# Moving two groups of transposes and turning the last two w2 products in a routed feed-forward kernel

## The chip, the core and the metric

The kernel runs on one core of one Trainium2 chip. A core has five engines with instruction queues of their own: TensorE (PE in the profile; PEld is its weight load) multiplies matrices and writes only to PSUM, a memory of eight banks of 512 fp32 values per partition; VectorE (DVE), ScalarE (ACT) and GpSimd (POOL) do elementwise work; SyncE (SP) issues DMA transfers, as POOL does for the indirect ones. Each engine runs its queue in order. The metric is the device time of one execution in microseconds (us). Less is better.

## The reference

Two layers work on x of shape (2, 1024, 512) in fp32. After every sublayer comes a layer norm of x plus the sublayer's output. Layer 0 is linear attention and a feed-forward with 4-bit weights, layer 1 is gated linear attention and a routed feed-forward. The change lies in the last of these, so only that is shown:

```python
scores = jnp.einsum('bsd,d->bs', hidden_states, router_weight) + router_bias[0]
top_scores, indices = jax.lax.top_k(scores, K)          # K = 512 of 1024 rows of a batch
weights = jax.nn.sigmoid(top_scores)
selected = jnp.take_along_axis(hidden_states, indices[:, :, None], axis=1)
h = jax.nn.gelu(jnp.einsum('bkd,df->bkf', selected, w1) + b1)      # 512 -> 2048
processed = jnp.einsum('bkf,fd->bkd', h, w2) + b2                  # 2048 -> 512
weighted = processed * weights[:, :, None]
out = flat.at[flat_idx].add(weighted.reshape(b * K, d))
...
x = _layernorm(x + _L1_ffn_ref(x, ...), axis=-1)
```

## The kernel before

The 2048 rows of x are four blocks of 512; two blocks are a batch of 1024. Everything lies in SBUF as tiles of 128 rows. A tile framework orders the instructions of each engine by when they were traced and what they depend on, and places the semaphores; `tc.issue_after(ins)` adds the order "behind `ins`" for the instructions of its block on `ins`'s engine. It is no wait of another engine. So the order on an engine is that of the scheduler, where nothing pins it.

*Routing* (`route`, a generator that is advanced with `next`). For each batch it has a column of scores (`score`) per 128 rows. Eight transposes (`rp`, L1320) spread them over all partitions, two ACT copies (L1321) make one row of 1024 scores. DVE then compares each of the eight columns with the row (L1329, L1332, L1335, the result in `cmp`) and counts how many are ahead: that is a row's rank. With the rank as an index, eight indirect DMAs (L1345, from POOL) scatter the rows of x into a DRAM buffer `picked`, where ranks of 512 and more fall away.

*Fetch* (`fetch`). One DMA (L1372, from SP) loads the 512 picked rows (`xs`); sixteen transposes (`xsTp`, L197), four to a bank, and four ACT copies (L1375) give them with the features on partitions. `sums_of_x` (L1382 to L1385) forms four sums T1 to T4 of them on DVE, since both feed-forward products are done by a scheme of seven half-size products instead of eight (Strassen's in Winograd's form).

*First product and gelu* (`hidden`, once for each of two batches). Four groups g of 512 hidden features; in each, seven products (`product`, L1407) of four fp32 matmuls of 128x256. A product goes to the next bank of `either_bank`, which takes one of the ring `mm_bank` (banks 0 to 3) and one of the ring `acc_bank` (banks 4 to 7) in turn; score rows and transposed rows take banks of the `mm` ring too. ACT takes the first product of a group (L1416), DVE adds the others (L1418 to L1424, and L1427 for the seventh), and ACT applies gelu (L1400) with the table load that comes before it. `beside[g]` holds functions that are traced behind a group's last sum: sums of w1 (`sums_of_w1`), the rest of the ranking of batch 1, and for group 3 of batch 0 `next_rows`, which fetches the rows of batch 1 and forms their sums.

*Second product* (`finish_ffn`, generator `steps(b)`). Again seven products (`add`, L1486, eight fp32 matmuls of 128x256 for each half r of a bank). At the end of a batch the fourth product, with T4, is added to p1 (L1561), and then rows are finished in tiles of 128: `to_x(i, half, y)` adds a half (256 columns) of tile i, weighted, to the row (L1532) and takes its statistics (L1533); `end(i)` aggregates these (L1537), normalises (`layernorm`: DVE L180, a power on POOL L181, DVE L183) and scatters the 128 rows to the output (L1539, indirect, from POOL). Tiles 1 and 3 need the fourth product, tiles 0 and 2 the third, with S1, which is last:

```python
nc.vector.tensor_add(p1, p1, product(of_h(b, 1, 1), of_T(T4)))
for r in range(2):
    ...
    end(2 * r + 1)
for r in range(2):
    p3 = either_bank("yp")
    add(p3, of_S(S1[b]), of_w2(1, 1), r)
    to_x(2 * r, 1, row_half(p3, r))
    end(2 * r)
```

[...]

Of the kernel before, what the change touches and what calls it, by code (L numbers as in the profile page):

```python
# [21 lines left out]
P = 128  # L22
# [51 lines left out]
def body(ctx: ExitStack, tc: tile.TileContext, a: dict, out: bass.AP):  # L74
# [627 lines left out]
    with tc.tile_pool(name="s2", bufs=1) as wk2:  # L702
# [137 lines left out]
        class Normed:  # L840
# [25 lines left out]
            def to_x(self, part):  # L866
                for i in part:
                    x = x_t[self.blk][:, i]
                    nc.gpsimd.tensor_add(x, x, self.y[:, i])
# [442 lines left out]
    def route(b, room):  # L1312

        s = score[b]
        row = room.rearrange("p k t -> p (k t)")[:, :T]
        for h in range(2):
            rp = mm_bank("rp")
            for i in range(4):
                col = s[:, 4 * h + i : 4 * h + i + 1]
                nc.tensor.transpose(rp[:, i * P : (i + 1) * P], col.to_broadcast([P, P]), ident)  # L1320
            nc.scalar.copy(row[:, h * 512 : (h + 1) * 512], rp)  # L1321
        cnt = sp.tile([P, 8, 3], F32, tag="cnt", name="cnt", bufs=1)
        nc.gpsimd.memset(cnt, 0.0)
        yield
        for i in range(8):
            col = s[:, i : i + 1]
            cmp = jk.tile([P, T], BF16, tag="junk", name="cmp")
            if i:
                nc.vector.tensor_scalar(  # L1329
                    cmp[:, : i * P], row[:, : i * P], col, None, ALU.is_ge, ALU.add, accum_out=cnt[:, i, 0:1]  # L1330
                )
            nc.vector.tensor_scalar(  # L1332
                cmp[:, i * P :], row[:, i * P :], col, None, ALU.is_gt, ALU.add, accum_out=cnt[:, i, 1:2]
            )
            nc.vector.scalar_tensor_tensor(  # L1335
                cmp[:, :P], row[:, i * P : (i + 1) * P], col, const("tril"), ALU.is_equal, ALU.mult,
                accum_out=cnt[:, i, 2:3],
            )
            yield
        rank = sp.tile([P, 8], F32, tag="rank", name="rank")  # L1340
        nc.vector.tensor_reduce(rank, cnt, AX.X, ALU.add)
        nc.vector.tensor_copy(index[b], rank)
        rows = []
        for i in range(8):
            ins = nc.gpsimd.indirect_dma_start(  # L1345
                out=picked[b][:, :],
                out_offset=bass.IndirectOffsetOnAxis(ap=index[b][:, i : i + 1], axis=0),
                in_=x_row[2 * b + i // 4][:, i % 4],
                in_offset=None,
                bounds_check=TOPK - 1,  # L1350
                oob_is_err=False,
            )
            apart(ins.ins, rows)
        yield
# [13 lines left out]
    def fetch(b, room=None):  # L1368

        xs = xT_tile("xs")  # L1370
        room = room or xT_tile("xsT")
        nc.sync.dma_start(out=xs, in_=picked[b].rearrange("(c p) d -> p c d", p=P)[:, :, :C])  # L1372
        for i in range(4):
            pt = transposed(xs[:, i], "xsTp")
            nc.scalar.copy(room[:, :, i * P : (i + 1) * P], pt.rearrange("p (k t) -> p k t", k=KC))  # L1375
        return xs, room
# [8 lines left out]
        nc.vector.tensor_sub(T3, B22, B12)  # L1385
        return (B11, B21, B22), (T1, T2, T3, T4)

    turns = [0]

    def either_bank(name):  # L1390
        turns[0] += 1
        return (mm_bank, acc_bank)[turns[0] % 2](name)

    def hidden(b, xs, h, beside):

        (B11, B21, B22), (T1, T2, T3, T4) = xs

        def gelu(f):
            x = h[f // 4][:, f % 4]
            nc.scalar.activation(x, x, AF.Gelu_apprx_tanh, bias=b1[:, f : f + 1])  # L1400

        def product(w, g, x):

            ps = either_bank("hp")
            for j in range(2):
                for k in range(2):
                    nc.tensor.matmul(  # L1407
                        ps[:, 256 * j : 256 * j + 256], w[:, k, 2 * g + j], x[:, k], start=k == 0, stop=k == 1
                    )
            return ps.rearrange("p (j t) -> p j t", j=2)  # L1410

        for g in range(4):

            c = h[g].rearrange("p (j e) (s t) -> p j e s t", e=2, s=2)
            c11, c12, c21, c22 = (c[:, :, e, s] for e in range(2) for s in range(2))
            nc.scalar.copy(c11, product(wA11, g, B11))  # L1416
            p2 = product(wA12, g, B21)
            nc.vector.tensor_add(c12, c11, product(wS2, g, T2))  # L1418
            nc.vector.tensor_add(c11, c11, p2)
            nc.vector.tensor_add(c21, c12, product(wS3, g, T3))  # L1420
            p5 = product(wS1, g, T1)
            nc.vector.tensor_add(c22, c21, p5)
            nc.vector.tensor_add(c12, c12, p5)
            nc.vector.tensor_add(c12, c12, product(wS4, g, B22))  # L1424
            for j in range(2):
                gelu(4 * g + 2 * j)
            ins = nc.vector.tensor_sub(c21, c21, product(wA22, g, T4)).ins  # L1427
            for j in range(2):
                gelu(4 * g + 2 * j + 1)
            if g in beside:  # L1430
                with tc.issue_after(ins):
                    beside[g]()
# [5 lines left out]
    def finish_ffn(w2, h):  # L1438
# [33 lines left out]
        def of_h(b, e, s):  # L1472
            return lambda r, j: hv[b][j // 2][:, j % 2, e, r, s]

        def of_S(x):
            return lambda r, j: x[:, j, r]

        def of_w2(e, half):
            return lambda j: w2v[j // 2][:, j % 2, e, 256 * half : 256 * half + 256]

        def of_T(x):
            return lambda j: x[:, j]

        def add(ps, x, w, r):
            for j in range(NJ):
                nc.tensor.matmul(  # L1486
                    ps[:, 256 * r : 256 * r + 256], x(r, j), w(j), start=j == 0, stop=j == NJ - 1
                )

        def product(x, w):  # L1490
            ps = either_bank("yp")
            for r in range(2):
                add(ps, x, w, r)
            return ps
# [3 lines left out]
        def steps(b):  # L1498
# [14 lines left out]
            with tc.issue_after(ins):  # L1513
# [10 lines left out]
                for i in range(4):  # L1524
                    x = xs[:, i]
                    nc.vector.scalar_tensor_tensor(x, b2, weight[:, i : i + 1], x, ALU.mult, ALU.add)
            stats = sp.tile([P, 4, 2, 6], F32, tag="stats", name="stats", bufs=2)

            def to_x(i, half, y):

                x = xs[:, i, 256 * half : 256 * half + 256]
                nc.vector.scalar_tensor_tensor(x, y, weight[:, i : i + 1], x, ALU.mult, ALU.add)  # L1532
                nc.vector.bn_stats(stats[:, i, half], x)  # L1533

            def end(i):
                mv = sp.tile([P, 1, 2], F32, tag="mv4", name="mv4")
                nc.vector.bn_aggr(mv[:, 0], stats[:, i])  # L1537
                layernorm(xs[:, i : i + 1], mv, 0.25e-5)
                ins = nc.gpsimd.indirect_dma_start(  # L1539
                    out=out[:, :],  # L1540
                    out_offset=bass.IndirectOffsetOnAxis(ap=place[:, i : i + 1], axis=0),
                    in_=xs[:, i],
                    in_offset=None,
                    bounds_check=B * T - 1,
                    oob_is_err=False,
                )
                apart(ins.ins, scattered)

            def row_half(y, r):
                return y[:, 256 * r : 256 * r + 256]  # L1550
# [7 lines left out]
            nc.vector.tensor_add(c11, p1, p5)  # L1558
            nc.vector.tensor_add(u2, u2, p5)
            yield  # L1560
            nc.vector.tensor_add(p1, p1, product(of_h(b, 1, 1), of_T(T4)))  # L1561
            for r in range(2):
                x = xs[:, 2 * r, 256:]
                nc.vector.scalar_tensor_tensor(x, row_half(u2, r), weight[:, 2 * r : 2 * r + 1], x, ALU.mult, ALU.add)
                to_x(2 * r + 1, 1, row_half(c11, r))
                to_x(2 * r + 1, 0, row_half(p1, r))
                end(2 * r + 1)
            for r in range(2):
                p3 = either_bank("yp")
                add(p3, of_S(S1[b]), of_w2(1, 1), r)  # L1570
                to_x(2 * r, 1, row_half(p3, r))
                end(2 * r)
            yield

# [122 lines left out]
    def x_room(i, name):  # L1697
        return xpool.tile([P, 4, ROW], F32, tag=f"x{i}", name=name)[:, :, :C]
# [3 lines left out]
    def rank_some(n):  # L1702
        for _ in range(n):
            next(ranking, None)

    def next_rows():
        xs, x = fetch(1, room)
        later.append(xs)
        later.append(sums_of_x(x, x_room(0, "xsums")))

    rank_some(4)
    hidden(0, xs, h[0], {0: lambda: (sums_of_w1((2,)), rank_some(6)), 1: lambda: sums_of_w1((3,)), 3: next_rows})
    h.append([xT_tile("h10"), part(3, [4, 512], "h11"), later[0], x_room(1, "h13")])
    hidden(1, later[1], h[1], {g: lambda g=g: unpicked(g + 1) for g in range(3)})
    finish_ffn(w2, h)
# [52 lines left out]
```

## Time and profile before

| what | before |
|---|---|
| median of 3 runs | 979.3 us (979.05 to 979.5) |
| the profiled execution's own time | 979.27 us |
| its span in the profile | 977.5 us |
| granted TensorE clock, mean | 0.997 |
| PE busy | 962.0 us, 98% |
| DVE busy | 707.6 us, 72% |
| ACT busy | 289.2 us, 30% |
| POOL busy | 305.4 us, 31% |
| first product (`hp`, two batches) | 770.2 to 872.1 us |
| second product (`yp`) | 872.1 to 968.8 us |

The profile is of one execution; its span starts with its first instruction, and 1.77 us lie around it. Times in views are us from the start of the span unless marked ns. A line of the timeline has start, length, engine, line, operation, tiles and shapes, and at its end the engine's idle time before it with the instruction that ended it. The chain of waits follows the last instruction back to what released it at each step.

### The profile page before, as it was taken

The numbers are of one execution on the slowest core, as the hardware profiler recorded it, in microseconds if no ns is written. First come the engines' busy times: TensorE is split into PE (matmuls) and PEld (weight loads), VectorE is DVE, ScalarE is ACT, GpSimd is POOL, SyncE is SP. The second block draws the span as 40 slices with busy tenths as digits, with TensorE's granted clock in tenths as the row PEclk, the third lists the DMA queues.
The fourth block names the chain that finished last, engine by engine and source line by source line (L and its number), as shares of the span: only waits on it lengthen the run. The fifth ranks groups of instructions, "written<-read, shape, count | busy, mean of one in ns | idle before, by whom it ended". The sixth has DMA issues, their size and how long they took to land. (4 is left out here: it accounts for less than half of the span.)

```text
span 977.5 us, 11854 instructions
## 1 busy us (share of the span) xinstructions
PE 962.0 (98%) x4421; PEld 776.0 (79%) x4421; DVE 707.6 (72%) x1347; ACT 289.2 (30%) x496; POOL 305.4 (31%) x276
## 2 busy tenths in 40 slices
PE   9999999999999999999999999999999999999996
PEld 6668876775888888888888879969768688888885
DVE  3569986987975686686578396655887794898544
ACT  2344323333642263253243223232122123220000
POOL 1110283004887265575567012001042021000022
PEclk9999999999999999999999999999999999999998
DMA  9622222100000000000020410000014302140011
GB/s 323 208 84 79 88 67 67 49 1 1 1 1 1 1 1 1 1 1 1 0 87 1 177 60 1 2 0 2 0 39 147 117 22 66 44 172 0 1 44 44
DMA packets 25980, 48.87 MB, mean 50 GB/s; under 512 B 4684, under 2 KB 6732, under 8 KB 25411
## 3 DMA queue, kind: packets, MB, share of 16 engines
q1 hardware_dynamic: 23283, 42.98, 13.2%
q0 software_dynamic: 1920, 4.22, 1.1%
q10 hardware_dynamic: 720, 0.92, 0.3%
q8 instruction: 35, 0.57, 0.2%
q14 instruction: 22, 0.18, 0.1%
HBM read 39.70 MB, written 10.52 MB: 51 GB/s over the span
## 5 line engine op out<-in xcount | busy, mean ns | idle before, releaser
L181 POOL TENSOR_TENSOR rs<-rs,table 128x4 f32<-128x4 f32 (+1 forms) x21 | 19.8, 946 | 312.2 <-DVE rs L180 311.9
L741 DVE SCALAR_TENSOR_TENSOR gate<-gatep,scale,gate 128x512 f32<-128x512 f32 x123 | 91.3, 743 | 6.4 <-PE gatep L730 6.1
L741 DVE SCALAR_TENSOR_TENSOR up<-upp,scale,up 128x512 f32<-128x512 f32 x112 | 83.0, 741 | 0.1
L730 PE MATMUL gatep<-x1Th,wgu 128*128 128x512 f32 x176 | 72.5, 412 | 0.6 <-DVE x1Tl L212 0.6
L730 PE MATMUL upp<-x1Th,wgu 128*128 128x512 f32 x176 | 70.4, 400 | 0.1
L730 PE MATMUL upp<-x1Tl,wgu 128*128 128x512 f32 x176 | 68.9, 392 | 0.0
L730 PE MATMUL gatep<-x1Tl,wgu 128*128 128x512 f32 x176 | 68.9, 392 | 0.0
L735 ACT ACTIVATE gate<-gatep,scale 128x512 f32<-128x512 f32 x41 | 28.3, 691 | 110.3 <-PE gatep L730 104.0
L777 PE MATMUL P<-wdn,h 128*128 128x256 f32 x256 | 60.5, 379 | 0.0
L931 POOL TENSOR_TENSOR h<-up,gate 128x512 f32<-128x512 f32 x30 | 38.6, 1287 | 68.6 <-ACT gate L930 63.3
L777 PEld LDWEIGHTS P<-wdn,h 128*128 128x128 f32 x256 | 48.4, 190 | 6.7
L1133 POOL TENSOR_TENSOR sum<-sum,sq 128x512 f32<-128x512 f32 x12 | 17.3, 1442 | 90.7 <-issue 75.9
L1163 PE MATMUL go<-big 128*128 128x256 f32 x192 | 43.4, 380 | 0.0
L367 PE MATMUL xk<-pair,x 128*128 128x512 f32 x96 | 42.7, 592 | 0.0
L730 PEld LDWEIGHTS upp<-x1Th,wgu 128*128 128x128 f32 x176 | 33.0, 188 | 11.7 <-DVE up L741 3.4
L188 DVE BATCH_NORM_STATS2 st<-x 128x6 f32<-128x512 f32 x64 | 41.9, 673 | 0.4
L730 PEld LDWEIGHTS gatep<-x1Th,wgu 128*128 128x128 f32 x176 | 33.1, 188 | 9.2 <-DVE gate L741 1.9
L1163 PEld LDWEIGHTS go<-big 128*128 128x128 f32 x192 | 36.2, 190 | 4.8
L730 PEld LDWEIGHTS upp<-x1Tl,wgu 128*128 128x128 f32 x176 | 33.1, 188 | 6.4 <-issue 0.2
L730 PEld LDWEIGHTS gatep<-x1Tl,wgu 128*128 128x128 f32 x176 | 33.1, 188 | 6.0
L777 PE MATMUL P<-T,S 128*128 128x256 f32 x160 | 36.0, 379 | 0.0
L777 PEld LDWEIGHTS P<-T,S 128*128 128x128 f32 x160 | 30.3, 190 | 4.2
(484 smaller groups left out, 2325.1 us busy)
## 6 DMA issues: line engine op xcount, KB each, us to landing
pk<-in_gu SPq DMA_DIRECT2D x16, 352.0 KB, 3.8
x<-in_x SPq DMA_DIRECT2D x4, 1024.0 KB, 13.1
w<-in_w SPq DMA_DIRECT2D x1, 4096.0 KB, 13.9
xs<-picked SPq DMA_DIRECT2D x4, 1024.0 KB, 4.9
out<-x SPq DMA_DIRECT2D x4, 1024.0 KB, 4.3
w<-in_w SPq DMA_DIRECT2D x4, 1024.0 KB, 6.9
x0T<-in_xT SPq DMA_DIRECT2D x3, 1024.0 KB, 7.2
pk<-in_dn SPq DMA_DIRECT2D x11, 256.0 KB, 3.3
```

Source lines behind the costliest of these rows:

```text
L181: power = nc.gpsimd.tensor_tensor(rs[:, :n], rs[:, :n], const("mhalf")[:, :n], ALU.pow).ins
L188: nc.vector.bn_stats(st, x)
L367: ins = nc.tensor.matmul(acc_of[b][c], x_t[blk][:, i, c * P : (c + 1) * P], pairs_of["k", blk][i // 2][:, i % 2], start=blk % 2 == 0 and i ...
L730: ins = nc.tensor.matmul(ps, wgu[:, k, at * P : (at + 1) * P], x[:, k], start=x is parts[0], stop=x is parts[1]).ins
L735: nc.scalar.activation(acc, ps, AF.Copy, scale=s)
L741: last = nc.vector.scalar_tensor_tensor(acc, ps, s, acc, ALU.mult, ALU.add).ins
L777: last_p[0] = nc.tensor.matmul(cut, x(j)[:, r], w[:, j], start=j == 0, stop=j == NP - 1 and tail is None).ins
L931: hm = nc.gpsimd.tensor_mul(h.chunk(f), up, gate).ins
L1133: nc.gpsimd.tensor_add(sum2, sum2, sq)
L1163: ins = nc.tensor.matmul(ps[:, 256 * m : 256 * m + 256], w[:, k, m], b[:, k, 256 * half : 256 * half + 256], start=first and m == 0 and k ...
```

## The change

Three places change. In `hidden`, every product is pinned behind the one before it on TensorE, and a function under `("last", g)` is traced ahead of the group's seventh product and pinned behind the sixth; the seventh is pinned behind it in turn. The score transposes of batch 1 (`first_ranks`) stand there in group 0 of batch 0, and the fetch of the rows of batch 1 (`next_rows`) in group 3; the sums of these rows (`next_sums`) stay behind the group. Before, the score transposes stood where the scheduler put them, between the first and the second matmul of the fifth product of group 0, and the row transposes behind the seventh product of group 3. In `steps`, the fourth and third product are computed half by half in turn (fourth r=0, third r=0, fourth r=1, third r=1), each half in a bank of its own. For the last half of batch 1, the third product is made of two pieces of 128 columns in two banks, each added to the row on its own, so that tile's row has three statistics instead of two.

The order of instructions moves with it: on ACT, gelus of groups 0 and 1 stand behind the next group's first copy, and the four copies of transposed rows stand together ahead of the gelus of group 3; on DVE, three adds of group 0 stand ahead of the comparisons instead of among them, and the seventh product's sum of group 0 (L1427) comes after the first three columns' comparisons; on POOL, power and output scatter alternate for all tiles. SP's order is the same.

```diff
@@ route
-                nc.tensor.transpose(rp[:, i * P : (i + 1) * P], col.to_broadcast([P, P]), ident)
+                last_turned[0] = nc.tensor.transpose(rp[:, i * P : (i + 1) * P], col.to_broadcast([P, P]), ident).ins
@@ hidden
-    turns = [0]
+    turns, last_hp = [0], [None]
...
             ps = either_bank("hp")
-            for j in range(2):
-                for k in range(2):
-                    nc.tensor.matmul(
-                        ps[:, 256 * j : 256 * j + 256], w[:, k, 2 * g + j], x[:, k], start=k == 0, stop=k == 1
-                    )
+            with tc.issue_after(last_hp[0]) if last_hp[0] else contextlib.nullcontext():
+                for j in range(2):
+                    for k in range(2):
+                        ins = nc.tensor.matmul(
+                            ps[:, 256 * j : 256 * j + 256], w[:, k, 2 * g + j], x[:, k], start=k == 0, stop=k == 1
+                        ).ins
+            last_hp[0] = ins
...
             nc.vector.tensor_add(c12, c12, product(wS4, g, B22))
+            if ("last", g) in beside:
+
+                with tc.issue_after(last_hp[0]):
+                    last_hp[0] = beside["last", g]()
             for j in range(2):
                 gelu(4 * g + 2 * j)
             ins = nc.vector.tensor_sub(c21, c21, product(wA22, g, T4)).ins
@@ steps
-            stats = sp.tile([P, 4, 2, 6], F32, tag="stats", name="stats", bufs=2)
-
-            def to_x(i, half, y):
-
-                x = xs[:, i, 256 * half : 256 * half + 256]
+            stats = sp.tile([P, 8, 6], F32, tag="stats", name="stats", bufs=2)
+            parts = {}
+
+            def to_x(i, half, y, n=256):
+
+                k = parts[i] = parts.get(i, -1) + 1
+                at = 256 * half
+                if n < 256:
+                    at += 128 * (k - 1)
+                x = xs[:, i, at : at + n]
                 nc.vector.scalar_tensor_tensor(x, y, weight[:, i : i + 1], x, ALU.mult, ALU.add)
-                nc.vector.bn_stats(stats[:, i, half], x)
+                nc.vector.bn_stats(stats[:, 2 * i + k], x)
...
-                nc.vector.bn_aggr(mv[:, 0], stats[:, i])
+                nc.vector.bn_aggr(mv[:, 0], stats[:, 2 * i : 2 * i + parts[i] + 1])
...
-            nc.vector.tensor_add(p1, p1, product(of_h(b, 1, 1), of_T(T4)))
             for r in range(2):
+                p4 = either_bank("yp")
+                add(p4, of_h(b, 1, 1), of_T(T4), r)
+                nc.vector.tensor_add(row_half(p1, r), row_half(p1, r), row_half(p4, r))
                 x = xs[:, 2 * r, 256:]
                 nc.vector.scalar_tensor_tensor(x, row_half(u2, r), weight[:, 2 * r : 2 * r + 1], x, ALU.mult, ALU.add)
                 to_x(2 * r + 1, 1, row_half(c11, r))
                 to_x(2 * r + 1, 0, row_half(p1, r))
                 end(2 * r + 1)
-            for r in range(2):
-                p3 = either_bank("yp")
-                add(p3, of_S(S1[b]), of_w2(1, 1), r)
-                to_x(2 * r, 1, row_half(p3, r))
+                if b == r == 1:
+
+                    for n in range(2):
+                        p3 = either_bank("yp")[:, :128]
+                        for j in range(NJ):
+                            nc.tensor.matmul(
+                                p3, S1[b][:, j, r], of_w2(1, 1)(j)[:, 128 * n : 128 * n + 128],
+                                start=j == 0, stop=j == NJ - 1,
+                            )
+                        to_x(2 * r, 1, p3, 128)
+                else:
+                    p3 = either_bank("yp")
+                    add(p3, of_S(S1[b]), of_w2(1, 1), r)
+                    to_x(2 * r, 1, row_half(p3, r))
                 end(2 * r)
@@ body, where the calls are
     def next_rows():
-        xs, x = fetch(1, room)
-        later.append(xs)
-        later.append(sums_of_x(x, x_room(0, "xsums")))
-
-    rank_some(4)
-    hidden(0, xs, h[0], {0: lambda: (sums_of_w1((2,)), rank_some(6)), 1: lambda: sums_of_w1((3,)), 3: next_rows})
+        later.extend(fetch(1, room))
+        return last_turned[0]
+
+    def next_sums():
+        later[1] = sums_of_x(later[1], x_room(0, "xsums"))
+
+    def first_ranks():
+        rank_some(4)
+        return last_turned[0]
+
+    hidden(0, xs, h[0], {("last", 0): first_ranks, ("last", 3): next_rows, 0: lambda: (sums_of_w1((2,)), rank_some(6)), 1: lambda: sums_of_w1((3,)), 3: next_sums})
```

## Prediction

> **What bounds the kernel now.** I read the page first, then TensorE's waits, then the chain of waits from 755 us to the end, and last the timeline around each place that the diff touches. The page:
>
> ```profile
> PE 962.0 (98%) x4421; PEld 776.0 (79%) x4421; DVE 707.6 (72%) x1347; ACT 289.2 (30%) x496; POOL 305.4 (31%) x276
> ```
>
> TensorE (PE) is busy 98% of the span of 977.5 us. So a change can only shorten TensorE's stream, fill its gaps, or shorten what follows its last product. Its waits from 770 us on are two:
>
> ```profile
> PE hp L1407 <- ACT row L1375: 1.1, 1, 1.1
> PE rp L1320 <- DVE score L1303: 0.9, 1, 0.9
> ```
>
> The chain shows where they lie, and that nothing but TensorE ends last between them (start, length, what):
>
> ```profile
> 778.55 1.09 PE rp L1320 x8
> 779.64 41.01 PE hp L1407 x190
> 820.65 0.45 PE xsTp L197 x4
> ...
> 823.00 0.49 ACT row L1375
> ...
> 823.53 48.61 PE hp L1407 x224
> 872.14 89.80 PE yp L1486 x416
> ```
>
> At 778.55 the score transposes wait for the scores. At 823.53 the first product of batch 1 waits for ACT's second copy of transposed rows, which stands behind two gelus (1.23 us from 821.77 in the same chain). After 823.53 TensorE runs gapless to 968.83. The tail follows:
>
> ```profile
> 961.76 7.07 PE L1486 MATMUL yp<-w,big 128*128 128x256 f32 x32
> ...
> 967.66 0.97 POOL L1539 DMA_INDIRECT out<-xs,place  x1 [0.30 <-DVE mv L1537]
> 968.65 0.59 POOL L181 TENSOR_TENSOR rs<-rs,table 128x1 f32<-128x1 f32 x1
> 969.27 0.55 DVE L183 TENSOR_SCALAR xs<-xs,mv,rs 128x512 f32<-128x512 f32 x1 [1.54 <-POOL rs L181]
> 969.73 0.48 DVE L1532 SCALAR_TENSOR_TENSOR xs<-yp,weight,xs 128x256 f32<-128x256 f32 x1
> ...
> 972.70 1.04 POOL L1539 DMA_INDIRECT out<-xs,place  x1 [0.87 <-DVE xs L183]
> ```
>
> TensorE is done at 961.76 + 7.07 = 968.83, yet DVE takes that result only at 969.73. It stood behind L183 of another tile, which waited for POOL's power, which waited for POOL's issue of the odd tiles' scatters. The last scatter is issued at 972.70; 4.8 us later the span ends.
>
> Steps used: a 256-column fp32 matmul is two records, 0.2157 apart (8 records take 1.89 with 0.379 for the last one); a transpose is one record, 0.109 apart (16 xsTp in 1.91).
>
> **Part 1, score transposes behind the sixth product of group 0.** Before, the last hp record ahead of them starts at 777.29, so the next could start at 777.50; it started at 778.55. That is 1.05, and the 8 transposes took 1.09 instead of 7 x 0.109 + 0.272 = 1.035: 1.10 to win. Behind 14 more records they start at 777.50 + 14 x 0.2157 = 780.52; the score is there since 778.50, and both banks are free by 779.1. So this gap closes.
>
> What is late next is the ranking. Before, rp start to DVE's first comparison was 1.80 (778.55 to 780.35, through two ACT copies), so it now starts at 782.32, 1.97 later. But three evictions (L1422, L1423, L1424 of before, 1.79 together) now stand ahead of the comparisons; before they lay among them at 785.04 to 787.43. DVE had no idle time from 780.35 to 798.59, so the add that ends this queue (L1419, group 1) starts at 782.32 + 18.24 - 1.79 = 798.77 and ends at 799.46, 0.18 later than before. One TensorE product waits for it: the third of group 2 takes the bank which that add empties.
>
> ```profile
> 798.59 0.69 DVE L1419 TENSOR_TENSOR h<-h,hp 128x512 f32<-128x512 f32 x1
> ```
>
> Before, the bank was free at 799.28, 0.49 ahead of the product (PE L1407 at 799.77). Now the product could start at 799.77 - 1.10 = 798.67 and is held to 799.49: 0.82, and some 0.1 for restarting (after the wait at 823.53, 16 records took 3.72, not 3.62). So 1.10 - 0.92 = **0.18 us** is left of part 1. No other wait in hidden or finish_ffn has under 2.8 us of room, the last product sums (T2, 0.7) apart, counted below. Bounds: 1.10 if the queue turns out 0.8 shorter; about -0.5 if DVE slips another 0.7. I take 0.18, since every row of that queue is in the trace.
>
> On ACT the gelus of groups 0 and 1 move behind the copies of the next group's first product. Their readers are the w2 products after 872; cover gone would need tens of us. The pins and the renamed stats places issue nothing.
>
> **Part 2, row transposes ahead of group 3's seventh product.** Same 16 transposes, 4 copies, one load; SP's and POOL's order stays. What changes is what TensorE does while ACT copies: 8 records (1.73) instead of nothing, and the copies no longer stand behind gelus. Before: 820.49 + 16 x 0.109 = 822.23 was possible, 823.53 happened: 1.30, with the restart 0.11 **1.41 us**. Room for the new order: rows must have landed; the timeline has the load's issue, the DMA view its size and us to landing:
>
> ```profile
> 811.47 0.37 SPq L1372 DMA_DIRECT2D xs<-picked  x1
> ```
>
> ```profile
> xs<-picked SPq DMA_DIRECT2D x1, 1024.0 KB, 5.0
> ```
>
> They land at 816.5, with the index 0.17 later at 816.7; TensorE gets there at 818.76 - 0.18 = 818.58. 1.9 us of room. Copies run from 819.27 at 0.48 each, the first is done at 819.9 and the second at 820.3; the seventh product takes the first one's bank at 820.3, and the second one's reader comes at 822.05. The xsums now queue behind the eviction of the seventh product (DVE 822.24 to 822.9), T2 is ready near 824.7, its product comes at 825.5. Before this room was 0.71, so it does not bind. Bounds: 0 (a wait of the same size appears at T2) and 1.41; I take 1.41.
>
> **Part 3, the w2 end.** Work in TensorE is the same but for the last product: 16 records of 256 columns become 32 of 128, with 8 more fp32 matmuls and their weight loads. [...] The row of the same form, with its weight loads:
>
> ```profile
> 73.64 3.69 PEld L418 LDWEIGHTS vk<-G,Wv 128*128 128x128 f32 x32
> 73.79 3.73 PE L418 MATMUL vk<-G,Wv 128*128 128x128 f32 x32
> ```
>
> (3.73 - 0.275) / 31 = 0.1115 a record, loads and products side by side. [...] The trace decides: 32 x 0.1115 - 16 x 0.2157 = **+0.12**.
>
> On the clock of before, the row-0 half of the fourth product ends at 958.47, the row-0 half of the third at 961.92 (its sums were done at 948.58), the row-1 half of the fourth at 965.37, and the quarters at 967.16 and 965.21 + 31 x 0.1115 + 0.275 = 968.94. The tiles thus end in turn 1, 0, 3, 2 and POOL's power and scatter alternate. Tile 1: POOL done by 963.6; tile 0: scatter about 965.1 to 966.2; tile 3: DVE takes its half at 965.41, aggregate 966.9, power 967.2, L183 967.85, scatter 968.7 to 969.75. The first quarter waits behind nothing, and DVE is free for the second at 968.98 instead of 969.73: 0.75. From there to the last scatter before took 972.70 - 969.73 = 2.97; the 128-element update costs 0.35 (comparison row of 128) against 0.48, the statistics of 128 some 0.30 (0.43 at 256, 0.69 at 512), the aggregate of three groups 0.03 more: 2.74. Last scatter 971.72 against 972.70: **0.98 us**, the +0.12 included. POOL must be free at 970.28 for the power; it is since 969.75. Batch 0 gets the same turns without a split: two adds of 0.41 for one of 0.69, beside DVE idle times of 6.5 and 2.5 us in that stretch; if that cover were gone, 0.2. Bounds for the tail: 0, if POOL's queue still sets the end, and 1.3.
>
> **Sum.** 0.18 + 1.41 + 0.98 = 2.57. The profiled execution took 979.27 (span 977.5 and 1.77 around it), the median is 979.3: the same. 979.3 - 2.6 = **976.7 us**. No change is within 0.2%, 977.3 to 981.3; that is about what a measurement of this kernel can tell.
>
> **The rivals.**
> 1. *The bank is free in time.* DVE's queue comes out 0.8 shorter and part 1 gives all of 1.10: 979.3 - 1.1 - 1.41 - 0.98 = 975.8. For it: 0.49 of room before. Against: DVE was gapless there.
> 2. *POOL still sets the end.* The scatters of tiles 3 and 2 run into each other, the tail gives nothing and the split costs 0.12: 979.3 - 0.18 - 1.41 + 0.12 = 977.8, no change. For it: each scatter holds POOL about 1.3 with its gap. Against: 0.5 of room worked out above.
> 3. *Slower: the pinned transposes outrun their rows.* They must now run before the seventh product, so a late load stops TensorE with ready work behind it. Decides from a landing 1.9 us later than worked out; each us more costs one, and 4.6 us of idling eats 2.6 and adds 2.0, the point from which it is slower. Here the clock counts: gaps of 1.05 and 1.30 left the granted clock at 1.00 in 775 to 785 and 815 to 830. [...] For it: ranking starts 1.97 later. Against: the three evictions pay it back, and the scatters and the load keep their durations.
>
> **How the numbers follow.** Main case 56% (976.1 to 977.3 as its pieces vary, nearly all of it faster), rival 1 12%, rival 2 17%, rival 3 8%; 7% for a mix, half of the gain lost, most of it under the limit. Faster by over 0.2%: 0.56 + 0.12 + 0.08 of the rest = 0.76. Within 0.2%: 0.16. Slower: 0.08. The range 975.9 to 978.3 leaves out rival 3 and the edge of rival 1.
>
> **What would show it.** Right: no TensorE wait at rp and at the first product of batch 1; a new wait of 0.7 to 1.0 us for DVE's second eviction of group 1 near 799.5; xsTp starting near 818.6; TensorE's end 1.5 us earlier; POOL alternating power and scatter, with under 8.2 us from TensorE's end to the span's end (8.7 before); quarter records 0.11 apart. Wrong: xsTp waiting for the DMA; quarters 0.2 apart; the last power waiting for a scatter.

## The result, and the profile after

The changed kernel takes 976.65 us (median of 15 runs, 975.34 to 977.48) against 979.09 (15 runs beside it, 978.33 to 979.77): a ratio of 0.9973, 95% interval 0.9966 to 0.9981. That is 2.4 us less. The profiled execution took 977.26 us, with a span of 975.5.

The page after, its first line and its busy times (share of the span, instructions):

```profile
span 975.5 us, 11890 instructions
PE 961.5 (99%) x4437; PEld 776.4 (80%) x4437; DVE 708.4 (73%) x1351; ACT 289.4 (30%) x496; POOL 306.4 (31%) x276
```

TensorE does as much as before (the sixteen more records of the last product cost 0.1), and the span is 2.0 shorter. So what went is idle time. TensorE's waits from 770 us on are now a single one, where there were two (total, times, longest):

```profile
PE hp L1408 <- DVE index L1342: 0.7, 1, 0.7
```

The chain of waits shows the same piece by piece (start, length, what):

```profile
771.03 10.36 PE hp L1408 x48
781.39 0.45 PE rp L1320 x4
...
799.39 0.09 DVE rank L1341
799.48 0.64 DVE h L1421
800.11 0.09 DVE index L1342
800.20 0.06 issue
800.26 19.23 PE hp L1408 x88
819.49 1.75 PE xsTp L197 x16
821.24 50.08 PE hp L1408 x232
871.31 93.24 PE yp L1492 x432
964.55 3.58 PE yp L1588 x32
968.16 0.36 DVE xs L1544
```

The score transposes (rp) follow the products without a gap, and so do the row transposes (xsTp) and the first product after them. In between, the chain leaves TensorE: from 781.87 to 800.20 it runs through ACT's copies and then DVE's whole ranking, and comes back through one product that waits for DVE. Two lines of the timeline say for what:

```profile
799.42 0.69 DVE L1421 TENSOR_TENSOR h<-h,hp 128x512 f32<-128x512 f32 x1
800.26 1.97 PE L1408 MATMUL hp<-big 128*128 128x256 f32 x8 [0.72 <-DVE index L1342]
```

The view names the index (L1342), because that is the last thing DVE finished before the product began. The index feeds POOL, not TensorE. What the product needs is the bank that the second add of group 1 (L1421) empties at 799.42 + 0.69 = 800.11; e8 below tells the two apart.

The tail, in the timeline:

```profile
964.39 3.73 PE L1588 MATMUL yp<-w,big 128*128 128x128 f32 x32
...
966.58 0.57 POOL L181 TENSOR_TENSOR rs<-rs,table 128x1 f32<-128x1 f32 x1 [1.37 <-DVE rs L180]
...
968.02 1.04 POOL L1551 DMA_INDIRECT out<-xs,place  x1 [0.87 <-DVE stats L1545]
968.16 0.35 DVE L1544 SCALAR_TENSOR_TENSOR xs<-yp,weight,xs 128x128 f32<-128x128 f32 x1 [0.23 <-PE yp L1588]
...
969.46 0.57 POOL L181 TENSOR_TENSOR rs<-rs,table 128x1 f32<-128x1 f32 x1 [0.40 <-DVE rs L180]
...
970.90 1.04 POOL L1551 DMA_INDIRECT out<-xs,place  x1 [0.87 <-DVE xs L183]
```

DVE takes TensorE's last result 0.04 after it is there (964.39 + 3.73 = 968.12, taken at 968.16; before it lay for 0.90). Power and scatter alternate on POOL, and the last power finds POOL idle. From TensorE's end to the last scatter it is 2.78 us, where it was 3.87.

To set traces beside each other they need a common zero. Executions differ by up to 1.6 us in their first 10 us, far ahead of anything that the change touches (the thirty-first TensorE record starts at 8.03 in e9 and at 9.65 in e5), and the first w1 product (hp) comes at 770.17 before and at 770.87 after. In the table all times count from each trace's own first hp record. "Time" is the median. "Ratio" is against the runs of the kernel before that were made beside each kernel (their medians: 979.32 for e1 to e4, 979.43 for e5 to e8, 979.41 for e9 to e11); it is not the quotient of the two medians, which would be 1.0018 for e6. The last scatter is the issue of the last output rows.

| kernel | time, us (runs) | ratio, 95% interval | xsTp starts | PE ends | last scatter |
|---|---|---|---|---|---|
| before | 979.09 (15) | 1 | 50.32 | 198.66 | 202.53 |
| changed | 976.65 (15) | 0.9973, 0.9966 to 0.9981 | 48.45 | 197.25 | 200.03 |
| e1, scores alone | 979.29 (11) | 0.9997, 0.9988 to 1.0006 | 50.18 | 198.52 | 202.37 |
| e2, rows alone | 978.08 (11) | 0.9987, 0.9978 to 0.9996 | 48.59 | 197.27 | 201.13 |
| e3, turns alone | 978.25 (11) | 0.9986, 0.9977 to 0.9995 | 50.32 | 198.78 | 201.54 |
| e4, no two pieces | 976.41 (6) | 0.9969, 0.9956 to 0.9981 | 48.45 | 197.13 | 200.13 |
| e5, w1 sums on POOL | 977.33 (11) | 0.9978, 0.9969 to 0.9987 | 47.50 | 196.29 | 199.06 |
| e6, more ahead of the add | 981.16 (11) | 1.0011, 1.0002 to 1.0020 | 52.26 | 201.05 | 203.82 |
| e7, scores behind the fifth | 976.38 (6) | 0.9969, 0.9957 to 0.9981 | 47.76 | 196.55 | 199.32 |
| e8, ranking split | 981.17 (11) | 1.0015, 1.0006 to 1.0024 | 51.23 | 200.06 | 202.83 |
| e9, POOL sums later | 975.91 (5) | 0.9965, 0.9952 to 0.9979 | 47.50 | 196.29 | 199.06 |
| e10, e7 and e9 | 975.54 (5) | 0.9964, 0.9950 to 0.9978 | 47.50 | 196.29 | 199.07 |
| e11, POOL sums beside the norm | 978.51 (11) | 0.9990, 0.9981 to 0.9999 | 49.58 | 198.38 | 201.15 |

By the last scatter the change gains 202.53 - 200.03 = 2.50. From there to the span's end it is near 4.78 us before and in e1, e2, e5, e9 and e11, and near 4.57 after and in e3, e4, e6, e7, e8 and e10. With the new `steps` both values occur, so the 0.2 is not put down to the change, and the last scatter is the better mark.

### The profile page after: what moved, and what is told of

The parts are those of the page before. It is cut to its first block, busy times and chain, and to the rows that moved or that the text cites. A ratio compares the mean times of both kernels' runs of the same rounds, so it can differ in the third digit from the quotient of the medians.

```text
span 975.5 us, 11890 instructions
## 1 busy us (share of the span) xinstructions
PE 961.5 (99%) x4437; PEld 776.4 (80%) x4437; DVE 708.4 (73%) x1351; ACT 289.4 (30%) x496; POOL 306.4 (31%) x276
```

## The experiments

### One part at a time (e1, e2, e3, e4)

The theory is the prediction's sum; the rivals are its rivals 1 (the bank is free in time, so the scores are worth 1.1) and 2 (POOL sets the end, so the turns are worth nothing).

e1 keeps the pins and the score transposes in their new place; row transposes and `steps` are as before:

```diff
-    hidden(0, xs, h[0], {("last", 0): first_ranks, ("last", 3): next_rows, 0: ..., 1: ..., 3: next_sums})
+    hidden(0, xs, h[0], {("last", 0): first_ranks, 0: ..., 1: ..., 3: next_all})   # rows and sums, as before
```

> Part 1 alone: score transposes pinned behind the sixth product of group 0, row transposes and the w2 end as before. Theory (the gain turns into a wait for the bank that DVE's queue empties): no wait at rp, a new TensorE wait of 0.7 to 0.8 us near 799.5 for DVE's second add of group 1, some 0.2 us faster than before, which a time cannot tell from no change. Rival (the bank is free in time): no new wait and 1.1 us faster. Second rival (ranking that starts 2 us later delays the rows): xsTp waits for the DMA and it is slower.

e2 keeps the pins and the row transposes; scores and `steps` are as before:

```diff
+    rank_some(4)
-    hidden(0, xs, h[0], {("last", 0): first_ranks, ("last", 3): next_rows, 0: ..., 1: ..., 3: next_sums})
+    hidden(0, xs, h[0], {("last", 3): next_rows, 0: ..., 1: ..., 3: next_sums})
```

> Part 2 alone: row transposes of batch 1 ahead of the seventh product of group 3, the rest as before. Theory: the wait of 1.1 at the first product of batch 1 is gone, the wait of 0.9 at rp stays, 1.4 us faster than before. Rival (the wait moves to the T2 sums, which now stand behind one more eviction): a new TensorE wait of about 1 us at the third product of batch 1, no change in time.

e3 has the new `steps`, with the last product's two pieces, and everything in `hidden` as before, without pins.

> Part 3 alone: last two w2 products by halves in turn, the last half of batch 1 in two banks, both transposes where they were before. Theory: TensorE ends as before or 0.1 later, the last scatter is issued 2.8 us after TensorE's end instead of 3.9, 1.0 us faster than before. Rival (POOL's queue sets the end): 3.8 us from TensorE's end to the last scatter, no change.

e4 is the changed kernel with the last half of the third product whole:

```diff
-                if b == r == 1:
+                if False:
```

> The changed kernel with the last half of batch 1 in one piece of 256 columns; the halves still go in turn. Theory (the turns free DVE and POOL before TensorE's end, the split itself only shortens the last update and statistics by 0.26 and costs TensorE 0.12): TensorE ends 0.1 earlier than in the changed kernel, the last scatter is issued 0.1 to 0.2 later, so the same time as the changed kernel to within 0.2 us and 2.4 us faster than before. Rival (the split carries the gain of the tail): 0.8 us or more slower than the changed kernel.

Measured: counted at the last scatter, e1 gains 0.16, e2 1.40 and e3 0.99. Together that is 2.55, and the whole change gains 2.50, so the parts add. The medians, against the 979.32 beside them, agree within what they can tell: nothing that can be told for e1, 1.2 for e2 and 1.1 for e3. TensorE's waits from 770 us on, first in e1 and then in e2:

```profile
PE hp L1408 <- ACT row L1375: 1.1, 1, 1.1
PE hp L1408 <- DVE index L1342: 0.7, 1, 0.7
```

```profile
PE rp L1320 <- DVE score L1303: 0.9, 1, 0.9
```

In e1 the wait for the scores is gone, and the wait named "index" stands in its place. It comes with the score transposes' new place alone. In e2 the wait for ACT's copies is gone, and no other one has come. So part 1 trades a wait for nearly the same wait, and rival 1 falls. Rival 2 falls with e3: TensorE ends 0.12 later there than before (the two pieces), and the last scatter is still 0.99 earlier.

e4 against the changed kernel: TensorE ends 0.12 earlier, and the last scatter is 0.10 later. So halving the last product costs 0.12 and gives back 0.22. The medians (976.41 with 6 runs, 976.65 with 15) can't tell 0.1. Nearly all of the tail's gain is in the turns.

### Is it the bank that DVE empties? (e5, e6, e7)

Theory: the product of group 2 waits for the bank which L1421 empties, and the ranking and w1 sums ahead of that add in DVE's queue set its time. The rival is the reading that the view's words suggest: TensorE waits for the ranking's index. In e5 four sums of w1 (group 2's, 2.4 us of DVE's queue) go to POOL:

```diff
-                ins = nc.vector.tensor_tensor(dst[:, :, j], x[:, :, j], y[:, :, j], op).ins
+                ins = by.tensor_tensor(dst[:, :, j], x[:, :, j], y[:, :, j], op).ins
...
-0: lambda: (sums_of_w1((2,)), rank_some(6))
+0: lambda: (sums_of_w1((2,), nc.gpsimd), rank_some(6))
```

> The changed kernel with the four w1 sums of group 2, which stand in DVE's queue between the comparisons (0.60 each), on POOL, which is idle there. Theory (the new wait is DVE's queue): the queue is 2.4 us shorter, the wait near 799.5 is gone, 0.8 to 0.9 us faster than the changed kernel, 975.8. Rival (POOL's sums of about 1.3 us each slow DVE or come too late for the wS2 product): the wait stays or another takes its place, no gain.

In e6 four more sums come ahead of the add:

```diff
-0: lambda: (sums_of_w1((2,)), rank_some(6)), 1: lambda: sums_of_w1((3,)), 3: next_sums
+0: lambda: (sums_of_w1((2, 3)), rank_some(6)), 3: next_sums
```

> The changed kernel with the four w1 sums of group 3 in DVE's queue ahead of the ranking too. Theory: the queue is 2.4 us longer and nothing covers it, the TensorE wait grows from 0.7 to 3.1 us, 2.4 us slower than the changed kernel, 979.1. Rival (slack elsewhere takes it): under 1 us slower. With a wait of 3.1 us the granted clock may drop behind it; if it does, 1 to 2 us more.

In e7 the score transposes stand eight records earlier, behind the product ahead of the sixth, so that the ranking begins sooner:

```diff
             nc.vector.tensor_add(c12, c12, p5)
+            if ("sixth", g) in beside:
+                with tc.issue_after(last_hp[0]):
+                    last_hp[0] = beside["sixth", g]()
             nc.vector.tensor_add(c12, c12, product(wS4, g, B22))
...
-("last", 0): first_ranks
+("sixth", 0): first_ranks
```

> The changed kernel with the score transposes pinned one product earlier, ahead of the sixth product of group 0 (TensorE gets there at 778.8, the scores are there at 778.5 on the clock of before). Theory: still no wait at rp, comparisons start 1.3 us earlier, the bank of the later product is empty at 798.7 when TensorE wants it at 798.7, so the wait shrinks from 0.7 to 0.1 or nothing: 0.8 us faster than the changed kernel, 975.8. Rival (part 1 has no more in it, the wait stays or comes back at rp): the same as the changed kernel.

Measured: the wait follows what stands ahead of that add. With 2.4 us less ahead of it (e5), or with the ranking begun 1.73 earlier (e7: rp at 8.63, not 10.36), TensorE has no wait above the view's limit left from 770 us on; e7 keeps one step of 0.400 instead of 0.216. With 2.4 more (e6), the wait is 2.4 longer:

```profile
802.75 3.36 PE L1408 MATMUL hp<-big 128*128 128x256 f32 x8 [3.13 <-DVE index L1342]
```

From the stage's start to the last scatter, e5 is 0.97 shorter than the changed kernel and e7 0.71. These three runs move index and add together, so they do not tell the two apart; e8 below does.

Two things did not come out of this sum. e5 is 0.97 shorter in the stage but not in time (977.33); that is taken up with e9. And e6 lost 3.79, not 2.4. The line above holds 8 records in 3.36 us, where the same eight take 1.97 after. The windows show why (stretch and length; busy time, with instructions in brackets, of PE, PEld, DVE, ACT and POOL; granted clock; DMA share; GB/s):

```profile
802.70:804.00 1.30, 1.25 (x3) 1.09 (x4) 1.20 (x3) 0.00 (x0) 1.02 (x1) 0.50 0.00 0
804.00:806.00 2.00, 2.00 (x7) 1.59 (x7) 1.86 (x4) 0.70 (x2) 1.39 (x3) 0.60 0.23 86
806.00:808.00 2.00, 2.00 (x11) 1.77 (x10) 1.50 (x3) 1.86 (x4) 1.55 (x2) 1.00 0.34 122
```

After a wait of 3.1 us the granted clock is 0.50, back at 1.00 from 806 on; the records come 0.427 apart instead of 0.216. Five steps of that size, with 0.559 ahead of them and 0.287 behind, make 1.4 more than the changed kernel's, and that is what was missing.

### What a late load would cost (e8)

Rival 3 had the pinned row transposes wait for their rows. e8 provokes it: the ranking's last two columns and the index move behind group 1's adds, so that the add comes early and the bank is free, and only index, scatters and load come later.

```diff
-0: lambda: (sums_of_w1((2,)), rank_some(6)), 1: lambda: sums_of_w1((3,))
+0: lambda: (sums_of_w1((2,)), rank_some(3)), 1: lambda: (rank_some(3), sums_of_w1((3,)))
```

> The changed kernel with the last two columns' comparisons and the rank moved behind group 1's last sum. Theory: the bank is free early, so the wait near 799.5 goes (0.8 won), but the index comes 3 us later, the rows land 3 us later, and the pinned row transposes wait some 2 us for the load: about 1.1 us slower than the changed kernel, 977.8. This is the price of rival 3 of the prediction: one us for each us of a late landing beyond its room. Rival (the load has more room than worked out): 0.8 us faster than the changed kernel.

Measured: the kernel is slower than expected, 981.17 us and not 977.8: the scatters come 4.70 us later and not 3, and six of the eleven runs lie in a group of their own (below). The bank wait is gone, although the first scatter of picked rows, which needs the index, starts at 34.31 from the stage's start instead of 29.61. That settles the reading of "index": with the add early and the index late, TensorE does not wait there. It waits later, for the rows (timeline; then the windows around it):

```profile
821.97 1.29 PE L197 MATMUL xsTp<-table,xs 128*128 128x128 f32 x10 [3.58 <-DMA xs<-picked]
```

```profile
822.00:824.00 2.00, 2.00 (x18) 1.98 (x19) 0.00 (x0) 1.31 (x3) 0.00 (x0) 1.00 0.02 4
```

TensorE, which without the bank wait gets to the transposes 0.95 earlier than in the changed kernel (47.50 in e9), stands there until 51.23. In the changed kernel the rows landed at 46.57 of the stage, 1.88 ahead of the transposes; here they land at 51.10, 4.53 later, and the transposes start 2.78 later. So beyond its room each us of a late load costs about one, as rival 3 said. The wait of 3.58 turned the gain into a loss: ratio 1.0015.

In this execution the clock stayed at 1.00 behind a wait longer than e6's. The windows on the two waits, e6's first:

```profile
799.50:802.70 3.20, 0.13 (x1) 0.00 (x0) 3.20 (x13) 0.00 (x0) 0.00 (x0) 0.92 0.00 0
818.00:821.90 3.90, 0.40 (x2) 0.00 (x0) 0.69 (x1) 0.00 (x0) 0.00 (x0) 1.00 0.89 264
```

In e6 TensorE was without work for 3.07 of these 3.20 us, and the clock fell within them. By the means of 0.92 here and 0.60 from 804 to 806 it was at 0.50 from about 802.2 to 805.6, for 3.4 us (an estimate). In e8 TensorE was without work for 3.50 of 3.90 us, and the clock was 1.00 throughout. So the length of a wait alone does not decide whether the clock falls; what else does is not shown.

The times of both kernels fall into two groups: e6's eleven times lie at 978.89 to 979.70 (five) and at 981.16 to 982.55 (six), e8's at 979.32 to 980.28 (five) and at 981.17 to 981.72 (six), with nothing between. e6's lower ones have a mean clock of 0.998 to 0.999, its upper ones 0.994 to 0.997. e8's do not part so: all six upper ones have 0.996, but so have three of the five lower ones, and the other two 0.998 (no run of the other experiments lies under 0.997). e6's profile is of the upper group, e8's of the lower. So the clock parts e6's two groups; what parts e8's is not shown.

### Why e5 lost in time what it won in the stage (e9, e10, e11)

In e5 the first w1 product comes 1.05 us later: the 120th TensorE record ahead of it starts 32.07 us before it, in the changed kernel 31.02, and the 60th 18.07 in both. So the loss lies in the attention stage, between 740 and 754. The POOL sums were pinned behind a DVE instruction, which orders nothing on POOL, and they ran in this stage. The timeline shows two of them beside DVE's normalization (POOL, then DVE):

```profile
745.96 1.26 POOL L1705 TENSOR_TENSOR big<-w 128x512 f32<-128x512 f32 x1
747.30 1.33 POOL L1705 TENSOR_TENSOR w<-w 128x512 f32<-128x512 f32 x1
```

```profile
746.02 3.80 DVE L183 TENSOR_SCALAR x<-x,mv,rs 128x512 f32<-128x512 f32 x4 [0.90 <-POOL rs L181]
```

These four take 1.91 in the changed kernel. One by one they start at 746.02, 747.43, 748.83 and 749.29: 1.41 apart while a sum runs, 0.46 without. TensorE then waited 0.78 for DVE (L1199) at 753.00. Theory: some DVE operations stand still while a POOL sum runs, as two of these four did. Rival: POOL's sums only came late. e9 puts the sums behind the scores, e10 does so in e7, and e11 puts them right beside the last normalization, whose four operations of line 183 would be 1.41 apart by the theory and 0.46 by the rival:

```diff
+    def sums_on_pool():                                                   # e9, e10
+        late = sp.tile([P, 8], F32, tag="late", name="late", bufs=1)
+        with tc.issue_after(nc.gpsimd.tensor_copy(late, score[1]).ins):
+            sums_of_w1((2,), nc.gpsimd)
...
+    def sums_on_pool():                                                   # e11; last_power: POOL's power in layernorm
+        with tc.issue_after(last_power[0]):
+            sums_of_w1((2,), nc.gpsimd)
...
-0: lambda: (sums_of_w1((2,)), rank_some(6))
+0: lambda: (sums_on_pool(), rank_some(6))
```

> The changed kernel with group 2's four w1 sums on POOL again, but queued there behind a small POOL copy of the finished scores, so that they run after about 780 in the expert stage and not in the attention stage as in e5. [...] DVE is relieved of 2.4 us and gives back 0 to 2.6; with one comparison held, TensorE's wait of 0.72 is gone and the time is 0.7 to 0.9 under the changed kernel, 975.8. [...]

> The same as e9, with the score transposes behind the fifth wait-free place of e7 (right behind the product that the sum wS3 feeds, before the sixth). No wait of TensorE is left in the stage in either theory; what stood in e7 as a single step of 0.400 instead of 0.216 us goes too. Theory: 0.8 to 1.0 us under the changed kernel, 975.7, and the picked rows' first scatter starts near 26 us from the stage's first product instead of 29.6. Since e7 alone already gives 0.70, it lies within 0.2 us of e7 and of e9: once no wait is left, relieving DVE more is worth nothing. Rival (DVE's load still sets the end): it is a further 0.5 us or more under e7.

> The changed kernel with group 2's four w1 sums on POOL right behind its power of block 3's normalization, so that they run from about 774.1 to 779.4, beside DVE's four normalizations of line 183 (0.54 us each) and four score products of line 1299 (0.68, two arrays in SBUF). [...]

e11 decides it (line numbers are three higher there, so L186 is L183 and L1708 is L1705; POOL first):

```profile
773.77 1.27 POOL L1708 TENSOR_TENSOR big<-w 128x512 f32<-128x512 f32 x1
775.12 1.33 POOL L1708 TENSOR_TENSOR big<-big,w 128x512 f32<-128x512 f32 x1
776.41 1.44 POOL L1708 TENSOR_TENSOR w<-w 128x512 f32<-128x512 f32 x1
777.82 1.45 POOL L1708 TENSOR_TENSOR big<-w,big 128x512 f32<-128x512 f32 x1
```

```profile
773.84 5.71 DVE L186 TENSOR_SCALAR x<-x,mv,rs 128x512 f32<-128x512 f32 x4 [1.12 <-POOL rs L183]
```

```profile
PE rp L1323 <- DVE score L1306: 1.7, 1, 1.7
```

Four normalizations, one for each sum, 1.41 apart; the scores come 3.8 later, the score transposes wait 1.7 us, and the last scatter is 1.12 later than in the changed kernel. By the rival e11 would have e9's time; it took 2.6 us more. In e9 the sums run from 777.92 to 783.00, and the attention stage is as in the changed kernel (the 120th record 31.02 ahead of the first product). The DVE operation beside the last sum keeps its 1.28:

```profile
781.49 1.28 DVE L1332 TENSOR_SCALAR_CACHE_REDUCE cmp<-row,score 128x1024 bf16<-128x1024 f32 x1 [0.42 <-ACT row L1321]
```

```profile
781.72 1.28 POOL L1705 TENSOR_TENSOR big<-w,big 128x512 f32<-128x512 f32 x1
```

The adds out of PSUM beside the other sums keep 0.68 too. No comparison of line 1335 was held: the first began at 782.96, as the last sum ended, and took 0.35, so one held, which the expectation allowed for, did not occur. In e5 it was not line 183 alone: two operations of line 1180 (two SBUF arrays) took 2.44 together from 756.01, with a sum on POOL from 756.44 to 757.91, and the next two 1.40. What the runs show is the standstill, and which operations it met; what holds them, and what parts line 183 from line 1332, is not shown.

e9 and e10 have no TensorE wait from 770 us on in the view, and end TensorE at 196.29 from the stage's start, 0.96 before the changed kernel. e10 starts the ranking 1.73 earlier than e9 and gains nothing by it in the trace. At 975.91 and 975.54 us both are the fastest here. By ratio they are not apart from each other, nor from the changed kernel by the intervals alone; that they are better than it rests on the trace, where the wait that is left of part 1 is gone.

## Why the prediction was right, point by point

**Part 1, 0.18.** e1 gained 0.16. The new wait was forecast at 0.82 with 0.1 for the restart. It was 0.88 and 0.08: the two steps of TensorE ahead of and behind its first record were 1.099 and 0.291 instead of 0.216. In the changed trace, less its late start of 0.70, the scores' transposes start at 780.53 (forecast 780.52), the first comparison at 782.28 (782.32), the add at 798.72 (798.77) and the product at 799.56 (799.49). What carried this was adding up the whole queue ahead of one add, not the gap that the edit closes: the gap alone would have said 1.10. That it came so close is partly luck, for two small errors offset in part: the add came 0.05 earlier than forecast, and the product started 0.15 behind its end instead of 0.03.

**Part 2, 1.41.** e2 gained 1.40. The transposes start at 818.63 (forecast 818.58), 1.9 us behind the landing of their rows, as forecast, and nothing waits at T2.

**Part 3, 0.98.** e3's last scatter is 0.99 earlier. The pieces' records are 0.1115 apart as in the row taken for it (32 in 3.73 us, loads beside them), and TensorE ends 0.12 later in e3, as forecast. They are not 0.2 apart, which would have shown the forecast wrong. Of the 0.98, 0.10 is the two pieces and the rest the turns; the prediction had not parted them.

**The sum, 2.57.** 2.50 by the last scatter, 2.4 by the medians. That the median hits the forecast 976.7 to 0.05 is luck, since the interval leaves 1.9 to 3.3 us. TensorE ends 1.41 earlier by the stage's own clock; "1.5 us earlier" was forecast.

**The rivals.** Rival 1 fell with e1, rival 2 with e3: POOL is free 0.40 ahead of the last power, where 0.5 was forecast. Rival 3 was real in kind and did not occur in the change: with the load made late by e8 the kernel is slower than before. Where it fell short is the clock: it puts the point from which the kernel is slower at "4.6 us of idling", and e6 shows a halving behind a wait of 3.1 us, at a cost of 1.4. By that cost a wait of some 3.2 us can make the kernel as slow as 4.6 did in the forecast (an estimate, 4.6 less 1.4), so the room of 1.9 us was less safe than it looked.

## What to carry to other kernels

When TensorE is nearly full, closing one of its gaps moves everything behind it forward, so ask which bank it reaches too early, and add up the queue of the engine that empties that bank. A wait line names the last event before the start, not the need: check which instruction releases the bank. Work given to POOL must be pinned on POOL's own queue, and kept away from DVE operations that stand still beside it, as line 183 did here.

## What the runs showed of the hardware that was not expected

- DVE stood still beside a POOL sum: line 183 came 1.41 us apart instead of 0.46, and exactly one went by for each sum (e5, e11), while a comparison out of one SBUF array (1.28) and the adds out of PSUM (0.68) kept their length (e9).
- Behind a wait of TensorE of 3.1 us the granted clock was 0.50 for about 3.4 us (e6), while a wait of 3.6 us left it at 1.00 in another execution (e8). e6's times fall into two groups about 2 us apart, and its mean clocks with them; e8's do so in time alone.
- From the last scatter to the end of the span it is 4.57 or 4.78 us, and with the new `steps` both occur.
